# Three bf16 passes for the f32 products of a causal attention layer, thirds made by GpSimd, and relative products stored in rows of 6 KB

## The chip, the cores and the metric

The kernel runs on one core of a Trainium2 chip, as one program and one launch. The metric is device time in microseconds, the median of the runs shown. The core has five engines that run side by side, each with its own queue in program order: TensorE (PE in the profile, PEld for its weight loads), VectorE (DVE), ScalarE (ACT), GpSimd (POOL), and SyncE (SP), which here issues nearly all DMAs. Matmuls write to PSUM[...].

## The reference

Four layers follow each other on 4 sequences of 1024 tokens with 128 features. Each computes `x = x + s * silu(f)`, with s from an attention or recurrent part and f from a feed-forward part on the layer-normed x. Only the last layer is changed. Its attention has 16 heads of 8 features, with a relative term, as the reference has it:

```python
ex = rel_embed[ns].reshape(n, NH, HD).transpose(1, 0, 2)
srel = srel_skew(jnp.einsum('bhnd,hmd->bhnm', qx, ex))
qk = (jnp.einsum('bhnd,bhmd->bhnm', qx, kx) + srel) * inv_dim
mask = 1000000000.0 * jnp.triu(jnp.ones((n, n), dtype=x.dtype), 1)
atten = jax.nn.softmax(qk - mask, axis=-1)
```

The reference names its shapes for 256 tokens and a table of 256 distances; on 1024 tokens the same table serves, and `srel_skew` shifts row n so that column m meets the row of the table for the distance between n and m. All inputs are f32. The feed-forward part has integer weights (hidden size 384).

## The kernel before

**Layers 0 to 2** keep x in SBUF; layer 2 leaves it in DRAM (`x3`). Nothing of their work is touched, but the constants that they read come from one tile, `const_sb`.

**Preparing layer 3** (`prepare3`, from L1628). Weights are transposed on PE. The table of distances, 256 rows, is padded by POOL so that the 8 features of each of four heads start at a multiple of 32 partitions (`spread`, L1619, and L1653), transposed into `W["emb"]`, and its first row subtracted from all (L1658 to L1661).

**Starting a sequence** (`begin3`, L1813). x is loaded in eight pieces, normed, transposed to `xnT`; the queries and keys of all heads are products of 512 tokens each (L1835), copied by ACT (L1836) and stored to DRAM as `qk` (L1837). Values go to `vd`. `project3` (L1876) loads a group's queries and keys, four heads at partitions 0, 32, 64 and 96 with 8 rows each; the two tiles come from a pool of two buffers, and POOL clears a first column of q for each group (L1881). `values3` loads values and copies them on POOL into `vb`, spread over the partitions of four heads.

**The order of the work.** The unit is a sequence b, a group i of four heads and a tile t of 128 queries; the tiles go in the order 7, 0, 6, 1, 5, 2, 4, 3 (`ORDER3`), so that long and short rows alternate. There are 4 x 4 x 8 = 128 units, and 12 score tiles of up to 512 keys in each group of 8 units, 192 in all. `layer3` (L1672) writes the program in a fixed pattern: products of the next score tile, transposes of an earlier unit, a piece of weighing, then the compare of the next score tile; at the end of a unit, one call of `relative3` for a unit seven ahead, pieces of the feed-forward part or of the next sequence (`beside`), and the load of distances for a unit three ahead (`ahead`). The framework's scheduler then settles the order on each engine and puts in the waits; it may move an instruction by some places.

**Relative products** (`relative3`, L1902). For a pair of query tiles and two heads, PE multiplies queries by `W["emb"]` into two PSUM tiles (tag "tr", three buffers that other small products share), ACT copies each to `r`, and SP stores it to a DRAM tile `flat` with rows of 384: 256 products, and the first 128 of them once more. A call makes four stores.

**Shear** (`shear3`, L1923). A read of `flat` with a row pitch one short of 384 puts each row's products where its distances belong. It fills two blocks of `rel` (the diagonal and one back). For tiles with t of at least 3, a second read fills the block three back. POOL then makes the blocks two and four back and the masked diagonal by `affine_select` (L1945) from the diagonal block.

**Scores** (`scores3`, L1958). For each of four heads one f32 matmul of 8 rows gives 128 queries by up to 512 keys; the four heads lie in four banks of one PSUM tile (tag "sc", one buffer). DVE adds the distances, scales, stores the negative to SBUF and keeps the minimum (L1986 and L1993); the exponential with its sum is ACT's (L2000). DVE transposes the weights in blocks of 32 (L1737), and `weigh3` multiplies them by the values (L2014), in PSUM tag "o". `finish3` divides by the sums, and `end3` makes the output projection of a sequence.

**Pools.** `l3` (one buffer for each tag), `l3d` (two), `l3r` (three buffers of one tag, "temp", which x, xn, qk, v, r, and the feed-forward's h and up share), and six DRAM buffers for `flat`.

Of the kernel before, what the change touches and what calls it, by code (L numbers as in the profile page):

```python
# [29 lines left out]
def _constants():  # L30
    i = np.arange(P)
    row, col = i[:, None], i[None, :]
    parts = []

    def rows(a):
        a = np.asarray(a, np.float32)
        return np.ascontiguousarray(np.broadcast_to(a.reshape(1, -1), (P, a.size)))

    parts.append(("ident", np.eye(P)))
    parts.append(("tri", row <= col))  # L40
    parts.append(("neg_ssd", np.where(col >= row, 0.0, -1e30)))
    parts.append(("tril", col < row))
    parts.append(("bd8", np.kron(np.eye(16), np.ones((8, 8)))))
    parts.append(("bd16", np.kron(np.eye(8), np.full((16, 16), 1.0 / 16.0))))
    parts.append(("ones", np.ones((P, P))))

    parts.append(("sel3", (row // 32 == col // 8 % 4) & (row // 8 % 4 == col // 32)))
    parts.append(("of_a", (row // 8 % 4) == np.arange(4)[None, :]))
    parts.append(("of_t", (row % 8) == np.arange(8)[None, :]))
    parts.append(("sel16", (row // 16) == np.arange(8)[None, :]))  # L50

    parts.append(("rep8", np.where(row < 8, (col % 8) == row, 0.0)))

    inv_freq = (np.float32(1.0) / np.power(np.float32(10000.0), np.arange(0, 8, 2, dtype=np.float32) / np.float32(8.0))).astype(np.float32)
    ang = (np.arange(T, dtype=np.float32)[:, None] * inv_freq[None, :]).astype(np.float32)
    tile_major = lambda a: a.reshape(NT, P, 4).transpose(1, 0, 2).reshape(P, NT * 4)
    parts.append(("cos", tile_major(np.cos(ang))))
    parts.append(("sin", tile_major(np.sin(ang))))
    parts.append(("kinv", rows(1.0 / np.arange(1, 17))))
    parts.append(("kidx", rows(np.arange(1, 17))))  # L60
    parts.append(("before", rows(np.tril(np.ones((8, 8)), -1))))
    parts.append(("freqs", rows(np.float32(1.0) / np.power(np.float32(10000.0), np.arange(16, dtype=np.float32) / np.float32(16.0)))))

    pick = np.zeros((P, 8, P))
    for e in range(8):
        pick[e : 24 : 8, e, :] = 1.0
    parts.append(("pick", pick.reshape(P, -1)))
    at, where = 0, {}
    for name, a in parts:
        where[name] = (at, a.shape[1])  # L70
        at += a.shape[1]
    return np.concatenate([np.asarray(a, np.float32) for _, a in parts], axis=1), where
# [20 lines left out]
class Kit:  # L93


    def __init__(self, tc, const, const_sb):
        self.tc, self.nc = tc, tc.nc
        self.const_sb = const_sb
# [6 lines left out]
    def c(self, name):  # L105
        at, n = CONST_AT[name]
        return self.const_sb[:, at : at + n]
# [1511 lines left out]
def spread(a):  # L1619

    return a.rearrange("p (i j r) -> p i j r", j=4, r=32)[:, :, :, 0:8]
# [6 lines left out]
def prepare3(k, w, W, ps):  # L1628
# [18 lines left out]
    W["emb"] = new("emb", [P, 4, 256])  # L1647
    with k.tc.tile_pool(name="pad3", bufs=1) as rp:
        pad = rp.tile([P, 2, 512], F32, tag="pad", name="pad")
        nc.vector.memset(pad, 0.0)  # L1650
        for c in range(2):
            for i in range(4):
                nc.gpsimd.tensor_copy(spread(pad[:, c, :])[:, i], heads_of(W["rel"][:, c, :])[:, i])  # L1653
        for i in range(4):
            k.transpose_tiles(ps, "tr", [pad[:, c, i * P : (i + 1) * P] for c in (0, 1)], W["emb"][:, i, :])

        e0 = rp.tile([P, 4], F32, tag="e0", name="e0")
        nc.vector.tensor_copy(e0, W["emb"][:, :, 0])  # L1658
        for i in range(4):
            nc.vector.tensor_scalar(W["emb"][:, i, :], W["emb"][:, i, :], e0[:, i : i + 1], None, op0=ALU.subtract)  # L1660
        nc.vector.tensor_scalar(W["emb"][:, :, 0], e0, -1.0, None, op0=ALU.mult)  # L1661
# [10 lines left out]
def layer3(k, W, x3, out, eps5, ps):  # L1672
# [12 lines left out]
    with ExitStack() as st:  # L1685
# [7 lines left out]
        def part(h):  # L1693

            at, h = divmod(h, 8)
            if at < 4 * NB:
                pair = ORDER3[h // 4 * 4 + h // 2 % 2] // 2
                if h % 2 == 0:
                    flats[at, pair] = dram.tile([2, 4, P, 384], F32, tag="flat", name="flat")
# [11 lines left out]
        batch[0] = {}  # L1711
# [9 lines left out]
        weights, transposes, weighs, out_of = {}, [], [], {}  # L1721
# [19 lines left out]
        def weigh(n):  # L1741
            nonlocal values
            b, i, t = units[n]
            at, pair = n // 8, t // 2
            if n % 8 == 2:
                out_of[at] = ps.tile([P, 8, 32], F32, tag="o", name="po")
            o = out_of[at]
            yield from weigh3(k, weights.pop((at, pair)), vb, o, pair)
            if n % 8 == 7:
                drain(values)  # L1750
# [18 lines left out]
        for x, (n, first) in enumerate(tiles + [(len(units), 0)] * 4):  # L1769
# [16 lines left out]
            if pos == 3 and i == 2 and b + 1 < NB:  # L1786
                batch[b + 1] = {}
# [7 lines left out]
            if pos == 6 and at + 1 < 4 * NB:  # L1795
                values = values3(k, p1, batch[(at + 1) // 4], vb, (at + 1) % 4)
                next(values)
            next(beside, None)
            ahead(n + 3)
# [13 lines left out]
def begin3(k, W, p1, p2, temp, ps, dram, x3, b, eps5, seq):  # L1813
# [4 lines left out]
    k.layernorm(p2, x.rearrange("p h a d -> p (h a) d"), xn, eps5)  # L1818
# [10 lines left out]
    seq["qk"] = dram.tile([2, P, T], F32, tag="qk", name="qk")  # L1829
    for n, name in enumerate(("WqT", "WkT")):  # L1830
        qk = temp.tile([P, T], F32, tag="temp", name="qk")
        for half in range(2):
# [3 lines left out]
            nc.scalar.copy(qk[:, tok], pp)  # L1836
        nc.sync.dma_start(out=seq["qk"][n], in_=qk)  # L1837
        yield
# [37 lines left out]
def project3(k, p2, seq, i, group):  # L1876

    nc = k.nc
    q = p2.tile([P, 1 + T], F32, tag="q", name="q")
    kk = p2.tile([P, T], F32, tag="k", name="k")  # L1880
    nc.gpsimd.memset(q[:, 0:1], 0.0)  # L1881
    group.update({"q": q, "k": kk, "sums": p2.tile([P, 4, NT], F32, tag="sums", name="sums")})
    for n, dst in ((0, q[:, 1:]), (1, kk)):
        for j in range(4):
            nc.sync.dma_start(out=dst[32 * j : 32 * j + 8], in_=seq["qk"][n, 32 * i + 8 * j : 32 * i + 8 * j + 8])
        yield
# [15 lines left out]
def relative3(k, W, temp, ps, flat, q, i, pair, jp):  # L1902
# [5 lines left out]
    r = temp.tile([P, 2, 2, 256], F32, tag="temp", name="r")  # L1908
    js = (2 * jp, 2 * jp + 1)
    pr = [ps.tile([P, 2, 256], F32, tag="tr", name="pr") for _ in js]  # L1910
    for m in range(2):
        for j, to in zip(js, pr):
            at, t = slice(32 * j, 32 * j + 8), 2 * pair + m
            nc.tensor.matmul(to[:, m, :], q[at, t * P : (t + 1) * P], W["emb"][at, i, :], start=True, stop=True)  # L1914
    for n, to in enumerate(pr):
        nc.scalar.copy(r[:, n], to)  # L1916
    rows = flat.rearrange("m j p u -> p j m u")
    for m in range(2):
        nc.sync.dma_start(out=rows[:, 2 * jp : 2 * jp + 2, m, 0:256], in_=r[:, :, m])
        nc.sync.dma_start(out=rows[:, 2 * jp : 2 * jp + 2, m, 256:384], in_=r[:, :, m, 0:P])  # L1920


def shear3(k, pool, flat, t):  # L1923
# [9 lines left out]
    shear = lambda n: bass.AP(base.tensor, base.offset + t % 2 * 4 * P * 384 + P, [(383, P), (P * 384, 4), (1, n)])  # L1933
    if t:
        nc.sync.dma_start(out=rel[:, :, slot(1) : slot(1) + 2, :].rearrange("p n s c -> p n (s c)"), in_=shear(256))
    else:
        nc.sync.dma_start(
            out=rel[:, :, 0, :], in_=bass.AP(base.tensor, base.offset + 2 * P, [(383, P), (P * 384, 4), (1, P)])
        )
    if t >= 3:  # L1940
        nc.sync.dma_start(out=rel[:, :, slot(3), :], in_=shear(P))
# [16 lines left out]
def scores3(k, p1, p2, ps, group, rel, t):  # L1958
# [8 lines left out]
    at = lambda j: slice(32 * j, 32 * j + 8)  # L1967
# [6 lines left out]
    for first in range(0, n, 512):  # L1974
        last = min(first + 512, n)
        sc = ps.tile([P, 4, 512], F32, tag="sc", name="score")
        for j in range(4):
            nc.tensor.matmul(  # L1978
                sc[:, j, 0 : last - first], q[at(j), 1 + t * P : 1 + n], kk[at(j), first:last], start=True, stop=True
            )  # L1980
# [93 lines left out]
def tile_kernel(ctx: ExitStack, tc: tile.TileContext, I, out):  # L2074
# [3 lines left out]
    n_const = CONST_AT["pick"][0]  # L2078
    const_sb = const.tile([P, n_const], F32, tag="const_sb", name="const_sb")
    nc.sync.dma_start(out=const_sb, in_=I["const"][:, 0:n_const])  # L2080
    k = Kit(tc, const, const_sb)
# [4 lines left out]
    whole = ExitStack()  # L2086
    xp = whole.enter_context(tc.tile_pool(name="x", bufs=1, side="right"))
# [57 lines left out]
```

## Time and profile before

| What | us |
|---|---|
| median of 3 runs | 3262.25 (3260.37 to 3266.85) |
| the profiled execution, its own time | 3261.59 |
| its span, first to last instruction | 3259.9 |
| busy in the span: PE, DVE, ACT, POOL | 2317.2, 2307.1, 1487.5, 1174.5 |
| last layer's loop, 2209 to 3236: span | 1027.00 |
| busy in it: PE, DVE, ACT, POOL | 862.89, 804.24, 624.58, 289.47 |
| exponentials, L2000 (512) | 390.0 |
| transposes, L1737 (512) | 362.0 |
| score products on PE, L1978 (1536 entries) | 295.0 |
| relative products on PE, L1914 (1024 entries) | 245.2 |
| weighing on PE, L2014 (10240 entries) | 242.9 |
| copies of relative products by ACT, L1916 (256) | 138.4 |

A group is a line of the kernel with one engine and one operation; its time counts overlapping instructions once. An f32 matmul leaves two entries on PE and two weight loads on PEld, so 1536 entries are 768 matmuls. In a timeline the columns are start, duration, engine, line, operation, out<-in, shapes and count, and in brackets how long the engine had been idle and what ended it. In a list of waits they are total, times, longest. The ends of matmuls are modelled, and a busy PE is not PE at its peak. "Granted clock" is the share of full speed that PE was allowed, and one digit of the row PEclk is its tenth in one of 40 equal slices of 81.5 us.

### The profile page before, as it was taken

To read this page: it belongs to the slowest core of one execution; us is meant where nothing else is said; L and a number is where in the kernel's file an instruction comes from. 1 tells how busy PE (TensorE), PEld (TensorE's weight loads), DVE (VectorE), ACT (ScalarE), POOL (GpSimd) and SP (SyncE) were. 2 spreads that over 40 slices of the span, in tenths; PEclk is the share of its full clock that TensorE was granted. 3 is DMA by queue.
4 is the path that set the end of the run, shared out by engine and by line. 5 is a ranking of instruction groups with operands and counts; after the bars stand their busy time and mean duration, and the time that the engine had idled before them with its cause. 6 is when DMAs were issued, how large, how long until landed. Compare 5 with 4: busy or idle time off the path is not lost. (4 is left out here: it accounts for less than half of the span.)

```text
span 3259.9 us, 50636 instructions
## 1 busy us (share of the span) xinstructions
PE 2317.2 (71%) x18321; PEld 1327.2 (41%) x18321; DVE 2307.1 (71%) x5534; ACT 1487.5 (46%) x3248; POOL 1174.5 (36%) x1104
## 2 busy tenths in 40 slices
PE   5787777677776777965533772557888888888885
PEld 2555555222322323651101222344545555555553
DVE  5555545878878886657868878437678778777786
ACT  4555453433333334344322561125665665755663
POOL 3344334144444444224577222332322322323322
PEclk9888888678788888985555666566766766756676
DMA  3000000100000000320433444347677677766772
GB/s 89 3 1 1 1 1 1 35 0 0 0 0 1 0 0 33 105 84 0 111 95 105 109 108 99 110 119 209 187 213 207 181 209 217 202 195 193 200 231 71
DMA packets 396446, 303.46 MB, mean 93 GB/s; under 512 B 96272, under 2 KB 380812, under 8 KB 390564
## 3 DMA queue, kind: packets, MB, share of 16 engines
q1 hardware_dynamic: 395044, 296.03, 32.2%
q10 hardware_dynamic: 1152, 4.19, 0.4%
q8 instruction: 144, 2.36, 0.3%
q14 instruction: 106, 0.87, 0.1%
HBM read 160.63 MB, written 138.94 MB: 92 GB/s over the span
## 5 line engine op out<-in xcount | busy, mean ns | idle before, releaser
L2000 ACT ACTIVATE neg<-neg,low 128x640 f32<-128x640 f32 (+7 forms) x512 | 390.0, 763 | 153.9 <-DVE low L1993 153.8
L1945 POOL TENSOR_SCALAR_AFFINE_SELECT rel<-rel 128x512 f32<-128x512 f32 x288 | 179.9, 637 | 565.6 <-DMA rel<-flat 357.3
L1737 DVE STREAM_TRANSPOSE wT<-neg 128x640 f32<-128x640 f32 (+7 forms) x512 | 362.0, 753 | 7.6 <-ACT neg L2000 6.9
L1978 PE MATMUL score<-k,q 8*128 8x512 f32 (+3 forms) x1536 | 295.0, 747 | 91.2 <-DVE low L1993 91.0
L1993 DVE CUSTOM_DVE_ANT_0 neg<-score,rel,low 128x128 f32<-128x128 f32 (+3 forms) x448 | 217.5, 516 | 152.5 <-PE score L1978 105.6
L1914 PE MATMUL pr<-emb,q 8*128 8x256 f32 x1024 | 245.2, 569 | 45.0 <-ACT r L1916 27.2
L2014 PEld LDWEIGHTS po<-wT,vb 128*32 128x32 f32 x10240 | 208.1, 140 | 143.3 <-issue 78.0
L2014 PE MATMUL po<-wT,vb 128*32 128x64 f32 (+1 forms) x10240 | 242.9, 259 | 31.7 <-issue 17.3
L1914 PEld LDWEIGHTS pr<-emb,q 8*128 8x128 f32 x1024 | 153.6, 269 | 124.4 <-ACT r L1916 62.9
L1916 ACT COPY r<-pr 128x512 f32<-128x512 f32 x256 | 138.4, 581 | 144.2 <-PE pr L1914 95.1
L1993 DVE CUSTOM_DVE_ANT_0 neg<-score,rel 128x512 f32<-128x512 f32 (+3 forms) x320 | 149.3, 520 | 26.7 <-issue 15.4
L1978 PEld LDWEIGHTS score<-k,q 8*128 8x128 f32 x1536 | 103.0, 249 | 153.9 <-DVE low L1993 127.8
L835 PE MATMUL pg<-xnT,w 128*128 128x512 f32 x256 | 148.4, 663 | 7.7 <-DVE h L839 4.5
L214 PE MATMUL pt<-ident,three 128*24 128x128 bf16 x64 | 9.2, 295 | 201.9 <-DVE three L211 201.9
L788 POOL TENSOR_TENSOR prod<-rest,kv 128x2048 f32<-128x2048 f32 x32 | 145.6, 4599 | 18.4 <-ACT rest L778 18.4
L837 PE MATMUL pu<-xin,w 128*128 128x512 f32 x256 | 140.5, 632 | 14.3 <-DVE h L839 7.9
L826 PE MATMUL po<-h,w 128*128 128x512 f32 x256 | 129.6, 627 | 27.1 <-DVE h L839 27.1
L838 ACT ACTIVATE h<-pg 128x512 f32<-128x512 f32 x128 | 75.9, 595 | 156.2 <-PE pg L835 152.7
L1986 DVE TENSOR_SCALAR_CACHE_REDUCE neg<-score 128x384 f32<-128x384 f32 (+2 forms) x192 | 79.7, 415 | 69.3 <-PE score L1978 69.3
L1050 PE MATMUL ph<-xin,upT 128*128 128x512 bf16 (+1 forms) x128 | 71.3, 588 | 78.5 <-DVE xin L1044 77.7
L1455 PE MATMUL read<-kt,const_sb 128*128 128x128 f32 x256 | 50.1, 366 | 94.2 <-POOL kt L1450 94.2
L431 PE MATMUL px<-hT,xbcT 128*128 128x512 f32 x256 | 115.4, 595 | 0.0
(621 smaller groups left out, 5690.5 us busy)
## 6 DMA issues: line engine op xcount, KB each, us to landing
flat<-r SPq DMA_DIRECT2D x256, 256.0 KB
rel<-flat SPq DMA_DIRECT2D x112, 512.0 KB
flat<-r SPq DMA_DIRECT2D x256, 128.0 KB
rel<-flat SPq DMA_DIRECT2D x96, 256.0 KB
kt<-kd SPq DMA_DIRECT2D x16, 512.0 KB
qt<-qd SPq DMA_DIRECT2D x16, 512.0 KB
kdc<-kdd SPq DMA_DIRECT2D x16, 512.0 KB
ktc<-ktd SPq DMA_DIRECT2D x16, 512.0 KB
```

What stands on the lines that cost most here:

```text
L788: nc.gpsimd.tensor_tensor(prod, attn.rearrange("p (t h g) -> p t h g", t=4, g=16)[:, t].unsqueeze(2).to_broadcast(each), kv[:, t, 1, :].re ...
L826: nc.tensor.matmul(po, W["w2"][:, e, c, :], h[:, c, :], start=(e == 0 and c == 0), stop=(e == 7 and c == 1))
L835: nc.tensor.matmul(pg, W["w1"][:, e, c * P : (c + 1) * P], xnT, start=True, stop=True)
L837: nc.tensor.matmul(pu, W["w3"][:, e, c * P : (c + 1) * P], xin, start=True, stop=True)
L1737: nc.vector.transpose(weights[at, pair][j][:, t % 2, 0 : (t + 1) * P], S[j][:, 0 : (t + 1) * P])
L1914: nc.tensor.matmul(to[:, m, :], q[at, t * P : (t + 1) * P], W["emb"][at, i, :], start=True, stop=True)
L1916: nc.scalar.copy(r[:, n], to)
L1945: nc.gpsimd.affine_select(out=rel[:, :, slot(back), :], in_=rel[:, :, slot(0), :], compare_op=op, fill=fill, base=0, pattern=[[0, 4], [-si ...
L1978: nc.tensor.matmul(sc[:, j, 0 : last - first], q[at(j), 1 + t * P : 1 + n], kk[at(j), first:last], start=True, stop=True)
L1993: nc.vector.tensor_tensor_reduce(out=neg[:, begin:last], in0=sc[:, j, begin - first : last - first], in1=rel[:, j, slot : slot + (last - b ...
L2000: nc.scalar.activation(neg[:, 0:n], neg[:, 0:n], AF.Exp, bias=here, scale=-1.0, accum_out=group["sums"][:, j, t : t + 1])
L2014: nc.tensor.matmul(o[32 * j : 32 * j + 32, 2 * pair + m.start : 2 * pair + 2, :], vb[:, kb, j].rearrange("p a d -> p (a d)"), weights[j][: ...
```

## The change

It has three parts, all in the last layer, and some that make room for them.

1. Queries and keys are split into three bf16 numbers each whose sum is the f32 number. `begin3` copies each product of 512 tokens to `rest`, and POOL makes the thirds: the upper half of the f32 word is the first, subtracted from the rest, and so twice. Queries are stored once, keys in three copies, so that the 8 features of a head become 24 rows: for each feature the three thirds of the query, against the same third of the key in all three rows. One matmul of 24 rows for each third of the key, three that add up in PSUM, takes the place of one f32 matmul of 8 rows. The same holds for the table of distances: its rows are tripled by POOL, and it is split by ACT and DVE.
2. `flat` becomes one tile of 128 rows by 4 heads by 2 query tiles by 384, and a call stores 6 KB for each partition with one DMA, where it made four stores. The 128 repeated products are written to `r` by a second ACT copy. Shears read with the new pitch.
3. The block three back is a copy on POOL of the block one back, where it was a second read of `flat`.

Beside these: the two tiles of queries are made once, and their first columns cleared once; the copy of the next group's values into `vb` is written after the load of distances (`fill_values`); the constants are split into a part that the last layer needs and a part whose space is freed before it.

On the engines, by the built programs: PE has 1536 relative and 2304 score matmuls for 512 and 768, each with a weight load of its own instruction; ACT 256 copies more, of 256 elements, and 3 of 1024; DVE 2 subtractions more; POOL 80 copies of `rel`, 64 instructions for thirds and 16 pad copies more, and 14 memsets fewer; SP 128 stores of `flat` for 512, and 80 loads of `rel` fewer.

```diff
@@ prepare3
-    W["emb"] = new("emb", [P, 4, 256])
+    W["emb"] = w.tile([P, 3, 4, 256], BF16, tag="emb", name="emb")
...
-                nc.gpsimd.tensor_copy(spread(pad[:, c, :])[:, i], heads_of(W["rel"][:, c, :])[:, i])
+                for a in range(3):
+                    nc.gpsimd.tensor_copy(spread(pad[:, c, :])[:, i, :, :, a], heads_of(W["rel"][:, c, :])[:, i])
...
+        for third in range(3):
+            nc.scalar.copy(W["emb"][:, third], emb)
+            if third < 2:
+                nc.vector.tensor_tensor(emb, emb, W["emb"][:, third], ALU.subtract)
@@ layer3
-                    flats[at, pair] = dram.tile([2, 4, P, 384], F32, tag="flat", name="flat")
+                    flats[at, pair] = dram.tile([P, 4, 2, 384], F32, tag="flat", name="flat")
...
+        qs = [p1.tile([P, 2 + T], BF16, tag=f"q{n}", name="q") for n in range(2)]
+        for q in qs:
+            nc.gpsimd.memset(q[:, 0:2], 0.0)
...
+        def fill_values():
+
+            while ripe:
+                drain(ripe.pop())
...
             if n % 8 == 2:
+                fill_values()
...
-                drain(values)
+                ripe.append(values)
...
+            ahead(n + 3)
+            fill_values()
             next(beside, None)
-            ahead(n + 3)
@@ begin3
-    k.layernorm(p2, x.rearrange("p h a d -> p (h a) d"), xn, eps5)
+    k.layernorm(p1, x.rearrange("p h a d -> p (h a) d"), xn, eps5)
...
-            nc.scalar.copy(qk[:, tok], pp)
-        nc.sync.dma_start(out=seq["qk"][n], in_=qk)
-        yield
+            three = temp.tile([P, 3, 512], BF16, tag="temp", name="three")
+            rest = temp.tile([P, 512], F32, tag="temp", name="rest")
+            nc.scalar.copy(rest, pp)
+
+            upper = rest.bitcast(BF16).rearrange("p (t two) -> p t two", two=2)[:, :, 1]
+            for third in range(2):
+                nc.gpsimd.tensor_copy(three[:, third], upper)
+                nc.gpsimd.tensor_tensor(three[:, 2] if third else rest, rest, three[:, third], ALU.subtract)
+            if name == "WqT":
+                nc.sync.dma_start(out=seq["q"][:, :, tok], in_=three)
+            else:
+                for a in range(3):
+                    nc.sync.dma_start(out=seq["k"][:, a, :, tok], in_=three)
+            yield
@@ project3
-            nc.sync.dma_start(out=dst[32 * j : 32 * j + 8], in_=seq["qk"][n, 32 * i + 8 * j : 32 * i + 8 * j + 8])
+        nc.sync.dma_start(out=q[32 * j : 32 * j + 24, 2:], in_=seq["q"][head].rearrange("d a t -> (d a) t"))
...
+        nc.sync.dma_start(out=kk[32 * j : 32 * j + 24], in_=seq["k"][head].rearrange("d a b t -> (d a) b t"))
@@ relative3
-            nc.tensor.matmul(to[:, m, :], q[at, t * P : (t + 1) * P], W["emb"][at, i, :], start=True, stop=True)
+        for third in range(3):
+            for j, to in zip(js, pr):
+                at = slice(32 * j, 32 * j + 24)
+                nc.tensor.matmul(
+                    to[:, m, :], q[at, first : first + P], W["emb"][at, third, i, :], start=(third == 0), stop=(third == 2)
+                )
     for n, to in enumerate(pr):
-        nc.scalar.copy(r[:, n], to)
...
+        nc.scalar.copy(r[:, n, :, 0:256], to)
+        nc.scalar.copy(r[:, n, :, 256:384], to[:, :, 0:P])
+    nc.sync.dma_start(out=flat[:, 2 * jp : 2 * jp + 2], in_=r)
@@ shear3
-        nc.sync.dma_start(out=rel[:, :, slot(3), :], in_=shear(P))
+        nc.gpsimd.tensor_copy(rel[:, :, slot(3), :], rel[:, :, slot(1), :])
@@ scores3
-        for j in range(4):
-            nc.tensor.matmul(
-                sc[:, j, 0 : last - first], q[at(j), 1 + t * P : 1 + n], kk[at(j), first:last], start=True, stop=True
-            )
+        for third in range(3):
+            for j in range(4):
+                nc.tensor.matmul(
+                    sc[:, j, 0 : last - first], q[at(j), 2 + t * P : 2 + n], kk[at(j), third, first:last],
+                    start=(third == 0), stop=(third == 2),
+                )
```

## The prediction

> **What bounds the kernel now.** The change lies in the last layer, so I first read the page, for where that layer begins and which engines it loads:
>
> ```profile
> span 3259.9 us, 50636 instructions
> ...
> PEclk9888888678788888985555666566766766756676
> DMA  3000000100000000320433444347677677766772
> ```
>
> From slice 27 on (2140 us) everything belongs to the last layer. Busy time by stretch (span, then PE, PEld, DVE, ACT, POOL, granted clock, DMA share):
>
> ```profile
> 2140.00:2209.00 69.00, 40.38 (x160) 29.08 (x160) 16.72 (x61) 19.86 (x39) 22.31 (x28) 0.62 0.55 157
> 2209.00:3236.00 1027.00, 862.89 (x13064) 542.21 (x13068) 804.24 (x2547) 624.58 (x1471) 289.47 (x414) 0.68 0.68 196
> ```
>
> So: a start of 69 us in which DVE works 17, and a loop of 1027 us in which DVE works 804 (78%), PE 863 (84%), ACT 625 (61%). Nothing is saturated. The waits of DVE in this layer (total, times, longest) say what fills its 223 us of idling:
>
> ```profile
> DVE neg L1993 <- PE score L1978: 111.3, 59, 9.7
> DVE neg L1986 <- PE score L1978: 69.3, 15, 25.2
> DVE neg L1993 <- issue: 42.5, 18, 6.8
> DVE neg L1993 <- POOL rel L1945: 13.9, 1, 13.9
> ```
>
> The 25.2 and the 13.9 belong to the start. In the loop DVE waits 111.3 + 69.3 - 25.2 = 155 us, 73 times, for products of queries and keys, and never for the distances. There is one score buffer in PSUM: a tile is PE's product, then DVE's compare, then the next product, with DVE's transposes beside it. A product costs time only where DVE has no transposes left, or where PE comes to it late, behind weighing, relative products or the feed-forward part. The DMA share of 0.68 is not on this path.
>
> In the timeline, eight entries are the four heads of one tile, f32, two entries for each matmul:
>
> ```profile
> 2706.04 0.71 PE L1978 MATMUL score<-k,q 8*128 8x256 f32 x8
> 2709.14 0.93 PE L1978 MATMUL score<-k,q 8*128 8x384 f32 x8
> 2719.10 0.81 PE L1978 MATMUL score<-k,q 8*128 8x128 f32 x8 [0.57 <-DVE low L1993]
> 2721.21 2.09 PE L1978 MATMUL score<-k,q 8*128 8x512 f32 x8 [1.30 <-DVE low L1993]
> ```
>
> The first two differ by 0.22 us for 128 columns, the last two by 1.28 for 384, 0.43 for 128: two speeds, 2:1, the four heads side by side. With the mean clock of 0.68, 36% of the work is at the fast one.
>
> **Part 1: three bf16 passes for f32 products.** The Trainium skill ("FP8 and Floating Point Precision", TensorE Precision Notes) has true FP32 as 4 passes through the array. By that rule alone a 512-column tile at the slow speed falls by a quarter, 2.09 to 1.57. The rows say less, for each pass now brings its own weight load: bf16 matmuls of 512 columns at the slow speed followed each other at 0.54 us (in the layer before, L1050 and L1037, with weight loads of 106 ns), 0.43 of columns (four times the 0.107 that the slope of 0.43 for 128 columns leaves to one of four passes, so the rule holds for the columns) and 0.11 of load that nothing hid. Three of these and the 0.18 that f32 has left after its two loads are 1.78 us slow and about 0.98 fast (for 1.14 in the timeline's fast tiles). I take the rows: 0.31 saved slow, 0.16 fast, 0.26 on the mean; by the same sum 0.17 for 384 columns, 0.08 for 256, none for 128. A group has 6, 2, 2 and 2 such tiles, there are 16: 96 x 0.26 + 32 x 0.17 + 32 x 0.08 = 33 us of PE. It reaches the end only in the 73 tiles for which DVE waits: 73 x 0.23 = **-17 us**. Bounds: -50 by the rule of a quarter everywhere (below), and +10 if 24 instructions for 8 entries are bound by issue.
>
> The relative products (L1914, 128 calls, 245 us): eight entries take 2.08 us in the timeline; six rounds of 0.213 (256 columns, one pass, slow) + 0.106 and the tail of 0.18 make 2.1. Between 0 and -0.2 us a call. That is PE time which mostly lies beside DVE: **-3 us**.
>
> **Part 2: rows of 6 KB.** ACT now writes the whole row, so two copies for one. The rows near it:
>
> ```profile
> L1916 ACT COPY r<-pr 128x512 f32<-128x512 f32 x256 | 138.4, 581 | 144.2 <-PE pr L1914 95.1 <-POOL x L228 16.0 <-issue 15.8
> L1866 ACT COPY up<-pgu 128x256 f32<-128x256 f32 x48 | 16.9, 375 | 0.0
> L1945 POOL TENSOR_SCALAR_AFFINE_SELECT rel<-rel 128x512 f32<-128x512 f32 x288 | 179.9, 637 | 565.6 <-DMA rel<-flat 357.3 <-DVE wT L1737 74.5 <-DVE low L1993 57.0
> ```
>
> 256 x 375 ns = 96 us more for ACT, from 61 to about 70% of the loop. Each copy frees one of three PSUM buffers for which PE's relative products wait, and the next score product stands behind these on PE. Today PE's weight loads wait 62.9 us for these copies, 48 times. Two copies of a call add up to 0.75 us to each: +36 at most, half of it +18. A part of PE's lateness is covered by DVE's transposes; I let half through: **+9 us** (bounds 0 and +50). The exponentials stand in the same ACT queue; DVE waits for them 6.9 us now, and I put that in the bound.
>
> Stores fall from 512 to 128, and the 80 extra loads of 256 KB go. In the loop that is worth nothing: POOL waits 357 us for these loads, but DVE never for POOL. The 80 copies on POOL instead (nearest row: 637 ns) are 51 us on an engine 28% busy, ahead of its selects: 0 while the loads come three units early, up to +10.
>
> **Part 3: thirds on POOL.** A half takes two copies (0.64) and two subtractions of 128x512 (1.06 to 1.27 on POOL, L1127, L227): 3.6 us; 16 halves are 58 us. The skill speaks against this place ("GPSIMD Engine Reference", 4.1 Engine selection: two-input elementwise work belongs on VectorE, GpSimd is about 2x slower). The rows agree only in part: DVE's subtraction would be 0.68 us, so four halves about 10.5 us there, 14.4 on POOL. For the 12 halves inside the loop POOL is right, DVE being the busier. ACT's copy of the next half waits for POOL to give its buffer back, with exponentials queued behind it, and POOL itself stands behind selects: **+7 us** over three batches (0 to +20). The moved fill of the values and the memset that goes (49.4 us of POOL's waiting) free POOL, which nobody waits for: 0. Loading the constants in two pieces: 0.
>
> **Part 4: the start.** Here nothing lies beside. Today:
>
> ```profile
> 2165.79 0.47 DVE L136 BATCH_NORM_STATS2 ln_st<-x 128x6 f32<-128x128 f32 x2
> 2174.89 0.59 ACT L1836 COPY qk<-pp 128x512 f32<-128x512 f32 x1 [1.48 <-PE pp L1835]
> 2181.80 1.34 PE L1914 MATMUL pr<-emb,q 8*128 8x256 f32 x4 [2.11 <-DMA q<-qk]
> 2186.90 0.62 SPq L1919 DMA_DIRECT2D flat<-r  x1
> 2203.16 0.51 SPq L1935 DMA_DIRECT2D rel<-flat  x1
> 2207.42 2.52 POOL L1945 TENSOR_SCALAR_AFFINE_SELECT rel<-rel 128x512 f32<-128x512 f32 x4 [15.52 <-DMA rel<-flat]
> 2208.69 0.35 DVE L1993 CUSTOM_DVE_ANT_0 neg<-score,rel,low 128x128 f32<-128x128 f32 x1 [13.91 <-POOL rel L1945]
> ```
>
> (a) Sixteen more pad copies at 0.207 on POOL, 3.3 us, ahead of the transposes of the table. Its thirds then stand ahead of the norm's statistics on DVE, as the order of the built program has it: copy, subtraction, copy, subtraction of 128x1024, about 1.1 and 1.2 each, 4.6. Statistics start 7.9 later. (b) The first copy of queries then ends at 2183.4. Four halves on POOL, 14.4, and 1 for buffers: 2198.8. On SP's queue the loads of queries stand behind the key stores and the store of values, whose ACT copies (1.2) wait for POOL: loads at about 2200 to 2202, relative products at 2203 for 2181.8, so +21. (c) Today 28 stores at 0.53 us hold SP from 2186.9 to 2203.2, which is 21.4 after the first relative product. Now seven stores follow ACT: 14 x 0.956 = 13.4, with lead and issue 16: -5. (d) Load and selects as now, plus one POOL copy: +0.6. Together **+16 us** (+10 to +24).
>
> **Sum.** Loop -17 - 3 + 9 + 7 = -4, start +16: +12 on the execution's own 3261.6 (3259.9 of span), 3273.6; the median of the runs is 0.7 above it: **3274 us**.
>
> **Rivals.** *PE's relief is worth the full quarter.* If the fixed parts shrink too, a quarter of the 155 us of waiting goes (-39) and of the lateness behind relative products (-12), ACT and POOL cost nothing, and the start +16: 3227. For it: the loop is a strict chain through one PSUM buffer, and PE is the busiest engine. Against it: the exposed bf16 loads. *ACT takes PE's place.* It goes to 70%, and PE's queue blocks behind a relative product that waits for a buffer. From the point where the two copies (1.9 us a call) outlast what PE has in its spare buffer, every call in the short units, half of 128, sends 0.75 us through: +48 - 20 + 16 = +44, 3306. For it: the 48 waits of today; against: 153.8 us in which ACT waits for DVE. *The passes bring nothing*: 24 instructions for 8 entries eat the saving, or PE, less busy, gets the slow speed more often (digits of 5 to 7 already): start +16 and beside +16, 3294.
>
> **Chances.** The forecast (3260 to 3288) 0.46, full relief 0.26, ACT 0.17, nothing gained 0.11. About 0.2% (6.5 us) can be told from no change. Faster: full relief without its upper edge, plus the forecast's lowest end, 0.27; same 0.13; slower 0.60. The range reaches from just below the relief case to the ACT case, 3222 to 3308; the forecast's own is 3260 to 3288.
>
> **What would show it.** Right: first compare of the layer about 16 us later, first relative product about 20; score tiles of 512 near 1.8 and 1.0 us; DVE's loop wait for PE near 135 us; ACT about 720 us busy in the loop, PE's wait for `r` up. Wrong: score tiles at 1.6 or below and DVE's wait near 100 (first rival); DVE waiting long for exponentials or for PE behind `r` (second); tiles as long as before, or a clock clearly below 0.68 (third).

## The result and the profile after

The changed kernel takes 3288.17 us (median of 4 runs, 3284.89 to 3291.31) where the kernel before took 3264.55 beside it (4 runs): a ratio of 1.0075, 95% interval 1.0061 to 1.0090, 0.75% slower. The profiled execution took 3287.11 us, 25.5 more than the one of before. From the page after, the answers to the rows shown of before:

```profile
span 3285.4 us, 52826 instructions
...
PEclk9888888688778878975656675556766766767676
DMA  3000000100000001211433453336567567567662
```

The start and the loop of the last layer, in windows as before (span, PE, PEld, DVE, ACT, POOL, granted clock, DMA share):

```profile
2140.00:2231.00 91.00, 39.29 (x196) 26.21 (x196) 18.25 (x59) 25.70 (x57) 37.92 (x56) 0.58 0.47 150
2231.00:3261.00 1030.00, 756.48 (x14319) 477.16 (x14322) 796.10 (x2547) 687.44 (x1713) 374.10 (x527) 0.69 0.63 189
```

The reader sees two things. The start has grown from 69 to 91 us. The loop is as long as before (1030 for 1027) although PE works 106 us less in it: ACT works 63 us more, POOL 85. In the two timelines the first compare with distances comes 22.1 us later (though what lies ahead of the layer took 0.9 less), from it to the end of the last are 2.7 more, and what comes behind takes 0.8 more.

The score tiles, twelve entries each now, show how large the relief of PE is:

```profile
2685.88 0.83 PE L2014 MATMUL score<-k,q 24*128 24x512 bf16 x12
...
2703.99 1.15 PE L2014 MATMUL score<-k,q 24*128 24x384 bf16 x12
2712.29 0.83 PE L2014 MATMUL score<-k,q 24*128 24x256 bf16 x12
```

512 columns take 0.83 at the fast speed (1.14 before), and at the slow one 1.47 (2.09 before; such a tile is shown below, at 2320.09); 384 and 256 columns at the slow speed take 1.15 and 0.83 (1.66 and 1.23). All 192 tiles are 196.2 us of busy time for 295.0.

VectorE's waits after:

```profile
DVE neg L2030 <- issue: 88.5, 24, 10.6
DVE neg L2030 <- PE score L2014: 62.3, 36, 10.1
DVE neg L2023 <- PE score L2014: 38.3, 1, 38.3
DVE wT L1753 <- ACT neg L2037: 31.4, 29, 4.7
DVE neg L2030 <- POOL rel L1980: 22.8, 4, 16.7
```

The 38.3 and 16.7 belong to the start. In the loop VectorE idles about as much as before (234 us for 223), but otherwise. The row "issue" names no releaser, so the waits were also summed tile by tile from the times of products and compares: VectorE idles while a product runs for 88.2 us (142.5 before), while PE comes late to a product for 108.7 (63.4), and between product and compare for 26.5 (10.7). The 54 us that shorter products give are spent again on lateness and on other waits.

ACT's two copies of each PSUM tile, where there was one:

```profile
L1953 ACT COPY r<-pr 128x512 f32<-128x512 f32 x256 | 151.2, 591 | 112.6 <-PE pr L1949 45.4 <-DMA flat<-r 31.0 <-POOL three L1861 21.7
L1954 ACT COPY r<-pr 128x256 f32<-128x256 f32 x256 | 98.2, 384 | 0.0
```

A copy begins before the one ahead of it has ended: copies that start at 2206.30, 2206.78 and 2207.04 us (first, second, next first) show that a second copy adds about 0.26 us to ACT's queue, and not its 0.38. For the 240 of the loop that makes 62 us, near the 63 that ACT works more.

The start, line by line:

```profile
2171.94 0.49 DVE L138 BATCH_NORM_STATS2 ln_st<-x 128x6 f32<-128x128 f32 x2 [1.17 <-ACT emb L1667]
...
2181.03 0.59 ACT L1856 COPY rest<-pp 128x512 f32<-128x512 f32 x1 [1.48 <-PE pp L1853]
...
2204.71 2.17 PE L1949 MATMUL pr<-emb,q 24*128 24x256 bf16 x18 [12.71 <-DMA q<-qd]
...
2209.64 13.65 SPq L1955 DMA_DIRECT2D flat<-r  x7
...
2223.39 0.39 SPq L1970 DMA_DIRECT2D rel<-flat  x1
...
2228.93 0.61 POOL L1976 COPY rel<-rel 128x512 f32<-128x512 f32 x1 [14.29 <-DMA rel<-flat]
...
2230.76 0.35 DVE L2030 CUSTOM_DVE_ANT_0 neg<-score,rel,low 128x128 f32<-128x128 f32 x1 [16.68 <-POOL rel L1980]
```

Statistics come 6.2 us later than before (2165.79), the first relative product 22.9, the first read of distances 20.2 (it follows the product by 18.7, not 21.4), and the first compare 22.1.

### The profile page after: what moved, and what is told of

Read it like the earlier page. It is cut to its first block, busy times and chain, and to the rows that moved or that the text cites. A ratio compares the mean times of both kernels' runs of the same rounds, so it can differ in the third digit from the quotient of the medians.

```text
span 3285.4 us, 52826 instructions
## 1 busy us (share of the span) xinstructions
PE 2212.1 (67%) x19599; PEld 1259.4 (38%) x19601; DVE 2302.1 (70%) x5536; ACT 1555.9 (47%) x3507; POOL 1276.7 (39%) x1250
## 5 line engine op out<-in xcount | busy, mean ns | idle before, releaser
L1753 DVE STREAM_TRANSPOSE wT<-neg 128x640 f32<-128x640 f32 (+7 forms) x512 | 368.7, 758 | 50.4 <-ACT neg L2037 31.4
L2014 PE MATMUL score<-k,q 24*128 24x512 bf16 (+3 forms) x2304 | 196.2, 433 | 105.6 <-DVE low L2030 101.7
L2051 PEld LDWEIGHTS po<-wT,vb 128*32 128x32 f32 x10240 | 198.3, 133 | 163.0 <-issue 96.5
L1949 PE MATMUL pr<-emb,q 24*128 24x256 bf16 x1536 | 202.2, 357 | 74.1 <-ACT r L1954 29.6
L1953 ACT COPY r<-pr 128x512 f32<-128x512 f32 x256 | 151.2, 591 | 112.6 <-PE pr L1949 45.4
L1976 POOL COPY rel<-rel 128x512 f32<-128x512 f32 x80 | 48.9, 611 | 345.9 <-DMA rel<-flat 298.5
L1949 PEld LDWEIGHTS <-q 24*128 24x128 bf16 x1536 | 120.9, 117 | 153.6 <-issue 81.8
L2014 PEld LDWEIGHTS <-q 24*128 24x128 bf16 x2304 | 67.8, 107 | 180.8 <-issue 149.3
L1457 PE MATMUL read<-kt,last_sb 128*128 128x128 f32 x256 | 49.4, 363 | 94.3 <-POOL kt L1452 94.3
```

The costliest lines, as they stand in the source:

```text
L1753: nc.vector.transpose(weights[at, pair][j][:, t % 2, 0 : (t + 1) * P], S[j][:, 0 : (t + 1) * P])
L1949: nc.tensor.matmul(to[:, m, :], q[at, first : first + P], W["emb"][at, third, i, :], start=(third == 0), stop=(third == 2))
L1953: nc.scalar.copy(r[:, n, :, 0:256], to)
L2014: nc.tensor.matmul(sc[:, j, 0 : last - first], q[at(j), 2 + t * P : 2 + n], kk[at(j), third, first:last], start=(third == 0), stop=(third ...
L2051: nc.tensor.matmul(o[32 * j : 32 * j + 32, 2 * pair + m.start : 2 * pair + 2, :], vb[:, kb, j].rearrange("p a d -> p (a d)"), weights[j][: ...
```

## The experiments

Each kernel ran beside the kernel before on one chip; "over before" is the difference of the two medians (3262.25 to 3265.01 for the one before). The loop runs from the first to the last compare with distances of the profiled execution. "FF groups" is what the four groups 1, 5, 9 and 13, in which the feed-forward part runs beside the scores, take together, each from the last compare of the group ahead to its own.

| Kernel | median | over before | ratio, 95% | first compare | loop | FF groups |
|---|---|---|---|---|---|---|
| before | 3264.55 | | | 2208.7 | 1027.2 | 281.6 |
| changed | 3288.17 | +23.6 | 1.0061 to 1.0090 | 2230.8 | 1029.9 | 289.7 |
| e1_rows | 3292.38 | +27.4 | 1.0049 to 1.0096 | 2208.4 | 1058.7 | 309.1 |
| e2_thirds | 3302.20 | +37.2 | 1.0095 to 1.0131 | 2229.3 | 1047.8 | 287.2 |
| e3_onecopy | 3268.46 | +3.4 | 0.9999 to 1.0018 | 2232.8 | 1010.3 | 276.2 |
| e4_beside | 3296.05 | +31.0 | 1.0075 to 1.0107 | 2234.2 | 1037.5 | 281.3 |
| e6_rows_onecopy | 3267.21 | +4.9 | 0.9999 to 1.0029 | 2211.2 | 1046.0 | 300.4 |
| e7_start | 3286.28 | +24.0 | 1.0058 to 1.0104 | 2229.3 | 1029.3 | 293.1 |
| e8_start_onecopy | 3268.35 | +6.0 | 1.0011 to 1.0029 | 2234.8 | 1016.0 | 275.8 |
| e9_onepass | 3298.44 | +36.1 | 1.0089 to 1.0134 | 2231.5 | 1038.6 | 292.8 |
| e10_best | 3260.43 | -1.8 | 0.9976 to 0.9995 | 2213.5 | 1025.7 | 283.5 |
| e11_order | 3270.25 | +8.0 | 1.0017 to 1.0037 | 2222.9 | 1019.2 | 279.9 |
| e13_onecopy_h | 3257.44 | -5.5 | 0.9967 to 0.9990 | 2233.7 | 999.1 | 256.5 |
| e12_best_h | 3241.67 | -21.3 | 0.9910 to 0.9952 | 2214.8 | 1005.0 | 261.7 |

The profiled execution of e6 took 3282.55, 15 us above its median, so its loop in the table is too long by about that; that of e8 lies 7.6 above.

**First theory**: in the loop shorter products are worth about what was forecast or more, and ACT's second copies take it back; the start loses to the thirds. Rival: VectorE bounds the loop, and neither counts.

**e1_rows**, rows of 6 KB without thirds (the shear, GpSimd's copy of the block three back and the split of the constants as in the changed kernel):

```diff
@@ relative3 of the kernel before
-        nc.scalar.copy(r[:, n], to)
...
+        nc.scalar.copy(r[:, n, :, 0:256], to)
+        nc.scalar.copy(r[:, n, :, 256:384], to[:, :, 0:P])
+    nc.sync.dma_start(out=flat[:, 2 * jp : 2 * jp + 2], in_=r)
```

> The kernel before with the 6 KB rows alone (two ACT copies of a PSUM tile, one store a call, the third block back copied by GpSimd); f32 products stay. My theory: ACT's second copies cost the loop 10 to 20 us, through late exponentials and PSUM buffers that come free late, and the start gains about 4 from fewer stores: 3270 to 3280, with DVE waiting 20 us or more for ACT's exponentials (6.9 in the kernel before). Rival (DVE is the loop's bound, so neither PE nor ACT counts): 3258 to 3262, the start's gain alone.

**e6_rows_onecopy**, the same with one copy and two stores:

```diff
-        nc.scalar.copy(r[:, n, :, 256:384], to[:, :, 0:P])
-    nc.sync.dma_start(out=flat[:, 2 * jp : 2 * jp + 2], in_=r)
+    nc.sync.dma_start(out=flat[:, 2 * jp : 2 * jp + 2, :, 0:256], in_=r[:, :, :, 0:256])
+    nc.sync.dma_start(out=flat[:, 2 * jp : 2 * jp + 2, :, 256:384], in_=r[:, :, :, 0:P])
```

> The kernel before with the 6 KB rows and GpSimd's copy of the third block back, f32 products, but one ACT copy for a PSUM tile and two stores a call. The rows with two copies made the loop 31.5 us longer (1058.7 for 1027.2). If ACT's second copies are that loss, the loop comes back to 1020 to 1030 and the kernel to 3256 to 3267. If it is the rows themselves (GpSimd's copies, or transfers that bunch), it stays at 1050 or more, 3283 to 3293.

Measured: +27.4 with two copies (12 us above the range expected), +4.9 with one. So ACT's second copies cost 22.5 us with f32 products (by the two intervals, about 9 either way), and rows of 6 KB with GpSimd's copy cost 5, by the interval 0 to 9. That answers the rival. The way was not the one expected: VectorE waited only 11.6 us for exponentials, and no start was gained. Of the 31.5 us by which e1's loop is longer than that of before, 27.5 lie in the FF groups, whose sums (first span, then PE, PEld, DVE, ACT, POOL) are, for before and for e1:

```profile
sum 282.00, PE 246.50 PEld 160.65 DVE 196.32 ACT 191.62 POOL 101.09; mean PE 61.63 PEld 40.16 DVE 49.08 ACT 47.90 POOL 25.27
```

```profile
sum 309.00, PE 273.42 PEld 175.76 DVE 195.26 ACT 207.57 POOL 105.32; mean PE 68.35 PEld 43.94 DVE 48.82 ACT 51.89 POOL 26.33
```

PE does the same work, but is busy 27 us longer: the granted clock of these four windows is 0.80 on the mean in before, 0.73 in e1. That the copies lower it is not shown: e6's profile, with one copy, has 0.75 and 300.4 us there, in an execution 15 us above its median. Over all runs the mean clock of an execution is lower with two copies than with one in both pairs (0.730 for 0.738 with f32 products, 0.736 for 0.741 in the changed kernel and e3), but whether a lower clock makes PE late or PE's waiting lowers the clock, no run separates. "TensorE: Matmul & The Clock Gate" of the Trainium skill (Part 1, What's actually happening) has a PE that pauses fall back to half its clock; the two speeds, 2:1, are in these traces, the pauses that set them were not traced.

**e3_onecopy**, the same edit as e6 on the changed kernel:

> The changed kernel with one ACT copy for a PSUM tile; the 128 columns that are repeated come from a second store of each call. My theory: ACT falls by about 95 us in the loop, exponentials come in time (DVE's wait for them from 31 to about 10 us), and the loop is 10 to 20 us shorter; the start changes by at most 3: 3268 to 3280. Rival (ACT has room enough, DVE or PE's other work bounds the loop): 3286 to 3290.

Measured: 20 us less than the changed kernel (+3.4 for +23.6), at the lower end of what the theory said; VectorE's wait for exponentials did not fall (34.3 for 31.4), so the stated way was wrong again. The FF groups went from 289.7 to 276.2.

**e2_thirds**, thirds with the four stores, the second read and the short rows of before:

> The changed kernel with stores, loads and shear of the kernel before: thirds and three bf16 passes alone. My theory: the start costs about 22 to 25 as before, but the loop keeps what the smaller products give, 10 to 20 us, since ACT makes one copy: 3267 to 3280. Rival (products aren't worth anything, DVE bounds the loop): start alone, 3285 to 3290.

Measured: 3302, slower than either theory allows. Its waits say why:

```profile
DVE neg L2032 <- POOL rel L1982: 21.3, 9, 10.0
...
DVE neg L2032 <- POOL vb L1932: 16.5, 2, 9.1
DVE neg L2032 <- DMA rel<-flat: 8.5, 3, 3.3
```

In the loop of the kernel before, VectorE never waited for distances; here it waits 46 us (16 in e3's loop), for distances and for the selects and value copies that stand in POOL's queue behind them. Keys go out three times and come back in 24 rows, beside the short rows: the DMA share is 0.73 (0.68 before, 0.69 in e3), and 968 issues hold SP's queue for 545 of 1047 us (647 issues and 409 of 1010 in e3). Whether the transfers or the queue that issues them make the distances late, no run separates. So the rows are not what the change pays for the thirds; they are what the thirds need. With one copy each, long rows and GpSimd's copy, against short rows and the second read, are worth 34 us (e3 against e2).

**e4_beside**:

```diff
+            next(beside, None)
             ahead(n + 3)
             fill_values()
-            next(beside, None)
```

> The changed kernel with the order of the kernel before in a unit: the piece of the feed-forward part or of the next batch stands ahead of the relative products and of the values, not behind them. If the lateness of products behind those pieces (about 60 us of DVE idling against 31 before) comes from the new order: 10 to 20 us shorter, 3268 to 3278. If it comes from the pieces themselves, on a PE whose score products now end earlier: within 4 us of the changed kernel, 3284 to 3292.

Measured: 7 us slower than the changed kernel. The order of the pieces is not what makes the kernel slow, although the FF groups alone are 8 us shorter in this profile (281.3 for 289.7).

**e9_onepass**:

```diff
-        for third in range(3):
+        for third in range(1):
```

> The changed kernel with one pass of bf16 in the products of queries and keys instead of three: it leaves out the two passes that add the lower parts of the keys, so the products are coarser. It prices PE's time in the loop: about 130 us of PE go, all in products that VectorE waits for 87 us in the loop. My theory (PE's relief is worth about half of the waiting that it removes, the rest comes back as lateness behind other work): 40 to 70 us less, 3218 to 3247. Rival (the loop is bound by VectorE and ACT, PE's time is worth nothing): less than 15 us, 3273 or more.

Measured: 12 us slower than the changed kernel (+36.1 for +23.6). But the experiment does not price PE's time, since the scheduler, given shorter products, built another order. ACT's loads of activation tables from 2200 us on (number, us in total, ns of one), in the changed kernel:

```profile
L2037 ACT ACT_TABLE_LOAD x17 | 21.8, 1283 | 0.3
L1894 ACT ACT_TABLE_LOAD x10 | 12.8, 1283 | 0.2
```

and in e9:

```profile
L2037 ACT ACT_TABLE_LOAD x33 | 42.3, 1283 | 0.6
L1901 ACT ACT_TABLE_LOAD x16 | 20.5, 1283 | 0.3
```

65 loads for 33 in all, 41 us more for ACT, since Silu and exponential now alternate more often. Yet VectorE waits only 6.7 us for exponentials (31.4 in the changed kernel). It waits for distances instead:

```profile
DVE neg L2030 <- POOL rel L1980: 58.3, 20, 8.9
```

In the changed kernel this row has 22.8, with 16.7 of it in the start. And the granted clock of the loop is 0.66 for 0.69. What the loads, the late distances and the clock cost apart is not shown. The run is inconclusive on its question, and shows that a program can get longer when a product gets shorter.

**e7_start**, a start with less of the thirds in it:

```diff
@@ prepare3
-            nc.scalar.copy(W["emb"][:, third], emb)
+            nc.gpsimd.tensor_copy(W["emb"][:, third], emb)
@@ begin3
+            eng = nc.gpsimd if b or name == "WkT" else nc.vector
```

(the table's subtractions move to GpSimd as well, the first sequence's halves lie in the buffers of the weights `wT`, and the query loads are written after the second query half)

> The changed kernel with another start and nothing else: the table's thirds by GpSimd alone, off VectorE's and ACT's queues; the first sequence's queries split by VectorE and its keys by GpSimd, in buffers of their own; the loads of the queries issued ahead of the key stores. My theory: table thirds (about 5 us), GpSimd's chain of four halves and the stores ahead of the query loads (about 12) are what the start costs: first compare 13 to 18 us earlier than 2230.8, the loop as it was (1030): 3269 to 3275. Rival (the start is set by stores and loads of the distances, not by the thirds): at most 5 us earlier, 3282 to 3287.

Measured: nothing gained; the rival was nearer. The profile of e7:

```profile
2173.67 0.49 DVE L138 BATCH_NORM_STATS2 ln_st<-x 128x6 f32<-128x128 f32 x2 [7.28 <-POOL emb L1667]
...
2196.62 2.16 PE L1960 MATMUL pr<-emb,q 24*128 24x256 bf16 x18 [8.37 <-DMA q<-qd]
...
2205.47 6.24 SPq L1939 DMA_DIRECT2D vr<-vd  x4
...
2211.81 9.93 SPq L1966 DMA_DIRECT2D flat<-r  x6
...
2221.83 0.41 SPq L1981 DMA_DIRECT2D rel<-flat  x1
```

The relative products do start 8 us earlier, but all of their stores except the first stand in SP's queue behind the key and value loads, and the first read is only 1.6 us earlier. And the statistics wait for the *last third of the table*, though GpSimd makes it now: the diff moves the norm's buffers from `l3d` to `l3` (`k.layernorm(p1, ...` for `p2`), which reuses the memory of the table's tile.

**e8_start_onecopy**, e7's start with one copy:

> The changed kernel with the other start and with one ACT copy for a PSUM tile (second store for the repeated columns). If the two causes are separate, their gains add: 3268.5 with one copy alone, less 13 to 18: 3250 to 3256, below the kernel before. If the loop takes back what the start gives (the same stalls later), 3263 or more.

Measured: +6.0, no better than e3's +3.4. Nothing to add up, since the start gave nothing.

**e11_order**, one copy, and only the order of SP's queue at the start changed; **e10_best**, that and e7's start, with the norm's buffers back in `l3d`:

```diff
-        drain(project3(k, p2, batch[0], 0, group[0]))
-        drain(values3(k, p1, batch[0], vb, 0))
-        for n in range(7):
+        project = project3(k, p2, batch[0], 0, group[0])
+        next(project)
+        for n in range(2):
             part(n)
-        for n in range(3):
+        ahead(0)
+        drain(project)
+        for n in range(2, 7):
+            part(n)
+        for n in range(1, 3):
             ahead(n)
+        drain(values3(k, p1, batch[0], vb, 0))
```

> The changed kernel with one ACT copy for a PSUM tile and only the order of SP's queue in the start changed: query loads, the first two stores of distances, their first read, key loads, the other stores, value loads last; all thirds where they were. By the new theory the first compare comes 10 to 15 us earlier than with one copy alone (2232.8), the kernel at 3254 to 3259. Rival: within 4 us of one copy alone, 3265 to 3270.

> The changed kernel with one ACT copy for a PSUM tile and a start built anew: besides the start tried before (table thirds by GpSimd, the first sequence's queries by VectorE and its keys by GpSimd), the norm's statistics get a buffer that doesn't overlie the table's, the first two stores of distances and the first read of them stand ahead of the key loads on SP's queue, and the value loads come last. New theory of the start: the relative products came 8 us earlier in the start tried before and the first compare only 1.5, since the stores stood behind key and value loads on SP's in-order queue, and the statistics waited for the last reader of the table whose memory they reuse. Then the statistics come at about 2167 (2172 in the changed kernel), the first compare at 2203 to 2213 instead of 2230.8, and the kernel takes 3240 to 3252. Rival (the round trip of the distances through DRAM, from store to select, is what sets the first compare, whatever the order): first compare at 2220 or later, 3258 or more.

Measured: the first compare comes 9.9 us earlier than in e3 by the order alone, and 19.2 by both; statistics at 2167.92 no longer wait. The theory of the start holds, or nearly (2213.5 where 2203 to 2213 was said). The time does not follow: e11 is 5 us slower over before than e3, e10 only 5 faster, and both miss the range that the theory gave. In e10, groups 0 and 1 take 54.9 and 76.4 us for 50.6 and 64.9 in e3 (group 0 from the end of its first four compares). What was won ahead of the loop waits at the next bound, group 1 with the feed-forward part.

**e13_onecopy_h and e12_best_h**, that part's product by VectorE, on e3 and on e10:

```diff
-                nc.scalar.copy(up[:, c, :], pgu[:, 1, :])
-                nc.gpsimd.tensor_tensor(h[:, c, :], h[:, c, :], up[:, c, :], ALU.mult)
+                nc.vector.tensor_tensor(h[:, c, :], h[:, c, :], pgu[:, 1, :], ALU.mult)
```

What the theory saw in the changed kernel is this stretch of its timeline, in group 1:

```profile
2320.09 1.47 PE L2014 MATMUL score<-k,q 24*128 24x512 bf16 x12 [0.94 <-DVE low L2030]
...
2322.48 0.35 ACT L1954 COPY r<-pr 128x256 f32<-128x256 f32 x1
...
2322.88 1.22 PE L1890 MATMUL pgu<-xnT,gateT 128*128 128x256 f32 x2 [1.32 <-ACT r L1954]
...
2323.60 1.28 ACT L1894 ACT_TABLE_LOAD   x1
...
2325.62 1.41 POOL L1896 TENSOR_TENSOR h<-h,up 128x256 f32<-128x256 f32 x2 [0.43 <-ACT up L1895]
...
2328.24 0.57 PE L1900 MATMUL po<-downT,h 128*128 128x128 f32 x2
...
2334.95 0.28 PE L2014 MATMUL score<-k,q 24*128 24x256 bf16 x1
...
2337.47 0.48 DVE L2030 CUSTOM_DVE_ANT_0 neg<-score,rel,low 128x256 f32<-128x256 f32 x1 [10.13 <-PE score L2014]
```

PE's first feed-forward matmul waits for ACT's second copy of `r` to free its PSUM buffer; Silu stands behind a table load; PE's down projection needs GpSimd's `h`; and the next score product stands behind all that. VectorE idles 10.13 us.

> The changed kernel with one ACT copy for a PSUM tile and the feed-forward part's product of gate and up by VectorE straight from PSUM: 48 ACT copies (about 17 us) and 48 products on GpSimd go, 48 products of 256 columns come to VectorE (about 17 us). If products of queries and keys come late in groups 1, 5, 9 and 13 (65 to 72 us each with one copy alone) because the feed-forward chain runs from ACT over GpSimd back to PE, ahead of them on PE's queue, these groups shorten by 3 or more each: 3250 to 3262. Rival (those pieces' own time on PE, or VectorE's time, is the bound): within 4 us or slower, 3265 to 3285.

> The kernel with the new start and one ACT copy, and the feed-forward product by VectorE straight from PSUM. If the chain over GpSimd is what took back the gain of the start in groups 0 and 1 (54.9 and 76.4 us, against 50.6 and 64.9 with the old start): 3240 to 3252. Rival (VectorE's 17 us count in full, or the loop takes the gain back elsewhere): 3258 or more.

Measured: both times as the theory said. The FF groups lose 20 us in e13 against e3 (276.2 to 256.5), although VectorE takes over some 14 us of work in them; three of the four lose 5 to 7 each, the first only 0.3, where 3 or more each was said. Their sums in e13:

```profile
sum 255.00, PE 205.08 PEld 138.66 DVE 206.55 ACT 179.53 POOL 73.92; mean PE 51.27 PEld 34.66 DVE 51.64 ACT 44.88 POOL 18.48
```

With the new start as well the kernel takes 3241.67 us, 0.69% less than before and 1.4% less than the changed one; group 1 takes 68.2 us for 76.4 in e10. Whether ACT's copies or GpSimd's place in the chain mattered more, these two runs don't separate: they take both away.

## Why the prediction was right, and where not

**The whole.** Slower was forecast, by 12 us; it is 24, and 3288.17 lies 0.2 past the upper end of the forecast's own 3260 to 3288. The split by stages was right: the loop about even (-4 forecast, +2.7 measured), the loss in the start (+16 forecast, +22.1 measured). Inside the loop two terms were both too small, and their errors cancelled: that the loop's sum came out is luck.

**Readings.** A mean clock of 0.68 between two speeds puts 36% of the time, not of the work, at the fast one. The 155 us of waiting left out the 42.5 of "issue": tile by tile, 206 of the 223 us went to products that ran or came late. And the 0.23 us of 73 x 0.23 has no working; 33 us over the 160 tiles that gain are 0.21.

**Products (-17, with relative products -3).** The step that failed is the choice of row. The bf16 matmuls of the layer before, one after the other with 0.11 us of weight load exposed, were no near row: here four heads lie in four row groups. A slow tile of 1.47 us is three times 0.43 of columns and the 0.18 left of the fixed part; no load shows at all, where 1.78 was forecast. So a slow tile gains 0.62 us, not 0.31. Relative products fell by 43 us of PE time (245.2 to 202.2), where 0 to 26 were forecast. "TensorE: Matmul & The Clock Gate" (Part 3, The mechanism) states that a weight load overlaps matmuls in flight only when the row group differs, which agrees, and would have decided between row and rule. With the thirds' own cost on GpSimd (+7 forecast) in it, the bf16 part of the loop is worth -23 to -26 by the pairs e6 and e3, e1 and changed (medians, less the difference of their starts), where the sum had -13. The first rival's premise was right: the tiles fell by a quarter and more, and the wait for products in the list fell to 62.3; but its 3227 did not come, since lateness and ACT's copies took the gain back.

**ACT's second copies (+9).** The term was mis-sized: 22.5 us with f32 products, 20 with bf16 (22 with e3's start set right), although ACT's work grew by 63 us and not by 96. I let half of 18 us through because transposes cover PE's lateness. In the FF groups, where most of it falls (13.5 us of the 19.6 between the loops of e3 and the changed kernel), that cover is gone where one chain goes through ACT's queue, as from 2320 to 2337 us. How much of the price came by this chain and how much with the lower clock stays open. The second rival (ACT takes PE's place) was right on the place, too high on the price.

**GpSimd's copies (0, up to +10)**: with the rows, 5, within what was said. **Stores and loads (0)**: wrong once there are thirds. With short rows and the second read the kernel would have taken 34 us more (e2 against e3).

**The start.** (a) 7.9 forecast, 6.2 measured (7.0 if the 0.9 is counted by which the layer begins earlier), but by memory as well as by queue: the statistics wait for ACT's last copy of the table. (b) The first relative product at 2203 forecast, 2204.7 measured. (c) The first read 16 after it forecast, 18.7 measured: ACT's copies of `r` waited up to 3.4 us for stores to free their buffers. (d) 0.6 forecast for GpSimd's copy, 1.8 measured from first read to compare. Together 16 against 22, (b), (c) and (d) all short.

**Rivals.** That the passes bring nothing gave 3294, the nearest time of the rivals, but for the wrong reason. A clock that falls because PE has less to do was not seen in the changed kernel (0.69 for 0.68); e9, with less work for PE still, has 0.66, from a cause that no run shows.

## What to carry to other kernels

Work out a shorter matmul from rows that lie in the array as it will, with the same row groups beside each other, and then ask which engine's small copies stand in the same PSUM rotation: here most of the 23 to 26 us that shorter products gave were paid back by 256 copies of 0.38 us. Look for the stretch where several in-order queues form one chain (here the feed-forward groups) and price added instructions there first: two thirds of what the copies cost in the loop fell there. A start won ahead of such a stretch is mostly lost until the stretch itself is mended: 19 us of start were worth 5 between e3 and e10, and 16 between e13 and e12.

## What was not expected of the hardware

In several kernels the granted clock goes with the time from run to run: e6 took 3253.3 to 3282.6 us in 22 runs, with mean clocks of 0.741 and 0.736 at these ends, and over the 22 runs 0.001 of clock went with 2.7 us (correlation -0.87); the kernel before has -0.73 to -0.88. It is no rule: over the 22 runs of e11 the correlation is -0.02. Which of the two, clock or time, follows the other is not shown. A single profile of this kernel can't settle 10 us. And VectorE and GpSimd slow each other when both split thirds: in e7 VectorE's copy of 512 elements took 0.43 us alone (at 2183.39) and 1.37 beside GpSimd's subtraction (at 2187.39), and that subtraction took 1.48, where a later one alone took 1.15.
